# Keys and values of three token groups computed in blocks of 64 tokens sorted by head, instead of for all heads

## The chip, the cores and the metric

The kernel runs on one core of one Trainium2 chip. A core has a matrix engine (TensorE, PE in the profile, with its weight loads as PEld), a vector engine (VectorE, DVE), a scalar engine (ScalarE, ACT), a general engine (GpSimd, POOL) and a sequencer for transfers (SyncE, SP). The engines run side by side, each works through its own instructions in order, and semaphores order them among each other. Transfers are issued from a queue (here SP's, and POOL's for indirect ones) and carried out by 16 DMA engines. The metric is the device time of one execution in microseconds.

## The reference

Six layers follow each other on 8 sequences of 256 tokens with 512 features, each as `x = layernorm(x + layer(x))`: a differential attention, a long convolution with the context, a mixture of experts, a self-attention, a cross-attention with the context, and a routed attention. The change is about the last:

```python
gating = softmax(x @ W_gate.T)                    # 16 heads
indicator = one_hot(argmax(gating), 16)
gating_top1 = indicator * max(gating)
q, k, v = split(x @ W_qkv.T, 3)                   # each 16 heads of 32
k_shared = einsum('bth,bthd->btd', indicator, k)  # the key of the token's own head
v_shared = einsum('bth,bthd->btd', gating_top1, v)
att = einsum('bhqd,bkd->bhqk', q, k_shared) / sqrt(32)
y = einsum('bhqk,bkd->bhqd', softmax(causal(att)), v_shared)
```

Queries are wanted for all 16 heads. Of keys and values each token needs only 32 + 32 columns, those of the one head that its gate picks; all heads of the attention then use this one key and value per token. All arithmetic is in float32, but for small terms that carry the row maxima.

## The kernel before

The 2048 tokens are 16 tiles of 128 (`x[0]` to `x[15]`, in SBUF all the time); four tiles (two sequences) are a group, so there are four groups (`NG`). `by_columns` writes one product of 128 x 512 as four matmuls, 32 columns of the stationary operand each (L202); a block of four such steps contracts 512 features. `feature_block` makes 128 query features of a group, transposed; `token_block` makes 512 columns for one tile of tokens.

**The loop.** `causal_attention` (L1210) runs 32 units in the routed stage, one for each sequence and 128-column block of heads (four heads). A unit passes through stages that lie several units apart: `maxima` (scores ps_q on PE, L1264; copied by ACT, L1273; masked by POOL, L1275; row maxima by DVE, L1284), `split` and `turn` once per four units (the maxima as three bf16 terms, turned by PE, L1306), `weights` (scores again with the maxima subtracted, ps_k, L1327 and L1336; exponential on ACT, L1344; mask and a sum on POOL, L1345 and L1355) and `products` (ps_pv, L1370 and L1380; reciprocal on DVE, L1388; scaling, L1394). ps_q and ps_k share one PSUM buffer.

**Order.** PE, DVE, ACT and POOL follow in this stage exactly the order in which the code is written. `prepare` hands each group's projections to a queue as steps with a planned cost and a due slot (a slot is a unit); `fill` takes steps from the queue between the parts of a unit, `need` takes those that are due, and `at(slots, place, f)` puts a function at the start, the middle or the end of a later slot, or into the queue. SP's instructions are ordered by the framework's own scheduler, by dependencies and priorities, not by the written order.

**Projections of a group** (`prepare` in `routed_attention`, L1794): four turns of tiles (PE, copied by ACT, L221 and L222); the gate (L178, L190) with its softmax and one-hot (`softmax_small`, `first_max`) on DVE; four query blocks; four key blocks and four value blocks for all 16 heads, each 16 matmuls into ps_t, of which DVE then chooses the token's own head: a product with the one-hot row (L1825) and a sum over heads (L1831). The chosen keys are repeated four times (L1836) and turned (L1841, L1844). Group 0's turns, gate, three queries and keys stand ahead of the first unit; the other groups' in the four units ahead of their own first, the values later.

**The stages ahead.** The expert stage already sends tokens to slots sorted by expert: POOL scatters rows with indirect DMAs (L882), SP loads blocks by register (L1022, L1030), and POOL gathers results (L1189). The regions xs and ys are zeroed in the first attention by `clear_slots` (L738), 16 transfers of 4352 KB from SP's queue. At the end of that attention `load_context` (L414) and `turn_context` bring the context tiles in, turn them and write them back (ctx_d, L419), two tiles ahead of PE. The cross-attention's last normalisations (L1742, L155) end where the routed stage begins.

Of the kernel before, what the change touches and what calls it, by code (L numbers as in the profile page):

```python
# [17 lines left out]
F32 = mybir.dt.float32  # L18
BF16 = mybir.dt.bfloat16
AF = mybir.ActivationFunctionType  # L20
ALU = mybir.AluOpType
AX = mybir.AxisListType
PSUM = bass.MemoryType.PSUM

P = 128
B, S, D = 8, 256, 512
NT = B * S // P
TPG = 4
# [18 lines left out]
NE = (PH * 2 * P - E * (P - 1) - 1) // P + 1  # L47


@with_exitstack  # L50
def decoder_kernel(ctx: ExitStack, tc: tile.TileContext, a: dict, out: bass.AP):
# [43 lines left out]
    ctx_d = dram.tile([P, KB, B * S], F32, tag="ctx_d", name="ctx_d")  # L95

# [146 lines left out]
    def turned_group(work, pools, g):  # L243

        xT = []

        def step(ti):
            if ti == 0:
                xT.append(work.tile([P, KB, GT], F32, tag="xT", name="xT", bufs=1))
            turned(pools, xT[0][:, :, ti * P : (ti + 1) * P], x[g * TPG + ti])  # L250

        return xT, [(0, [(TR, lambda ti=ti: step(ti))]) for ti in range(TPG)]
# [439 lines left out]
    def experts(rt):  # L692
# [39 lines left out]
        def clear_slots(pool):  # L732
# [3 lines left out]
            for e in range(E):  # L736
                for region in (xs, ys):
# [5 lines left out]
                    )  # L743

# [461 lines left out]
        return clear_slots, load_experts, load_gu_last, router, blocks, combine, wide  # L1206
# [577 lines left out]
    def routed_weights(w):  # L1784
        g = 3 * D * KB
        load_w(w, g, a["L1_ffn_W_gate"], H1)
        nc.vector.memset(w[:, g + KB * H1 : g + KB * H1 + 32 - H1], 0.0)
        return load_w(w, 0, a["L1_ffn_W_qkv"], 3 * D), w[:, g:]

    def routed_attention(wqkv, wg):  # L1790

        idx = index_row(const, H1, "idx_h")

        def prepare(work, pools, g, at, here):  # L1794
# [5 lines left out]
            k4 = work.tile([P, TPG, 4, HD1], F32, tag="k4", name="k4")  # L1800
            ind = work.tile([P, TPG, H1], F32, tag="ind", name="ind")
            itop = work.tile([P, TPG, H1], F32, tag="itop", name="itop")

            part = work.tile([P, GT], F32, tag="gpart", name="gpart", bufs=1)

            def gate_parts():
                columns_by_block(
                    pools.tile([P, GT], F32, tag="mm", name="ps_g"), part, wg, H1, lambda k: xT[0][:, k, :]
                )

            def gates():
                pt = pools.tile([P, TPG, P], F32, tag="mm", name="pt_g")
                gate = work.tile([P, TPG, H1], F32, tag="gate", name="gate")
                sum_of_blocks(gate, pt, part)
                softmax_small(work, gate, H1)
                top = work.tile([P, TPG], F32, tag="top", name="top")
                first_max(work, gate, H1, idx, top, ind)
                nc.vector.tensor_tensor(
                    itop, ind, top.unsqueeze(2).broadcast_to([P, TPG, H1]), ALU.mult
                )  # L1820
# [12 lines left out]
            def key(ti, ps):  # L1833
                k = k4[:, ti]
                chosen(k[:, 0, :], ps, ind[:, ti, :])
# [9 lines left out]

            xT, need = turned_group(work, pools, g)
            need.append((0, [(MM, gate_parts)]))
            need.append((0, feature_block(pools, qT, xT, wqkv, 0, 0, HD1**-0.5)))
            need.append((0, [(TR, gates)]))
            need.append((0, feature_block(pools, qT, xT, wqkv, 0, 1, HD1**-0.5)))  # L1850
            for ti in range(TPG):
                need.append(
                    (0, token_block(pools, xT, wqkv, D, ti, lambda ps, ti=ti: key(ti, ps)))
                )
            need.append((0, feature_block(pools, qT, xT, wqkv, 0, 2, HD1**-0.5)))
            need.append((0, [(TR, keys_turned)]))
            for c in range(3, KB):
                need.append((c, feature_block(pools, qT, xT, wqkv, 0, c, HD1**-0.5)))
            for ti in range(TPG):
                need.append(  # L1860
                    (
                        5 + ti // 2 * (4 if g == NG - 1 else 2),
# [142 lines left out]
```

## Time and profile before

| | us |
|---|---|
| median of 3 runs | 2131.78 (2131.77 to 2133.14) |
| the profiled execution: time | 2132.13 |
| its span on the core | 2130.4 |
| routed stage (end of the cross-attention's PE work to the end of the span) | 347.8 |
| of it ahead of the first unit | 34.0 |
| PE busy in the routed stage | 307.1 |
| DVE busy there | 243.0 |

A row of a timeline gives start, duration, engine, line and operation, `out<-in`, and in brackets the idle time ahead of it and who ended it. A float32 matmul stands as two records in the profile, so 16 matmuls are 32 records. A row of a group gives the count after an x, then busy time and the mean of one in ns, then the idle time of the engine ahead of it with the releaser. A row of a DMA gives the number of transfers, KB of each, and the median time from issue to landing. `granted clock` is the share of PE's full clock.

### The profile page before, as it was taken

Reading aid. Unit: us, or ns where it says so; the run is one execution under the profiler, and the core shown is the slowest. Engines: PE = TensorE matmul, PEld = TensorE weight load, DVE = VectorE, ACT = ScalarE, POOL = GpSimd, SP = SyncE. Lnnn points to the kernel's source line nnn. Section 1 sums busy time; section 2 is a strip of 40 time slices with the busy share of each in tenths; the row PEclk is TensorE's granted clock in tenths of the full one; section 3 lists DMA queues with packets and bytes.
Section 4 is the critical chain, followed back from the end, with each engine's and each line's share of the span. In section 5 each row is a group of like instructions: output and inputs, shape, how many; then the busy total and the mean of one; then the engine's idle time right before and its main releaser. Section 6 shows DMA issues by size and latency. Waiting matters only on the chain. (4 is left out here: it accounts for less than half of the span.)

```text
span 2130.4 us, 46282 instructions
## 1 busy us (share of the span) xinstructions
PE 1985.9 (93%) x20206; PEld 1127.1 (53%) x20206; DVE 1272.5 (60%) x1935; ACT 604.1 (28%) x765; POOL 828.1 (39%) x919
## 2 busy tenths in 40 slices
PE   8979999879998999999969999998999999999995
PEld 5545555434443446656535554547787874344443
DVE  4677777658888964222235766565334343577787
ACT  4555555520010013211114433430110111333342
POOL 2677777637556833000034554332000000242443
PEclk9999999999999999999989999999999999999998
DMA  6899902235124145142132211002100100000000
GB/s 226 320 398 390 351 4 62 85 93 197 30 80 150 48 126 180 64 144 70 43 102 62 91 61 32 2 2 100 40 26 15 40 0 1 1 8 15 11 22 31
DMA packets 110073, 198.24 MB, mean 93 GB/s; under 512 B 7088, under 2 KB 30768, under 8 KB 109872
## 3 DMA queue, kind: packets, MB, share of 16 engines
q1 hardware_dynamic: 104752, 178.49, 24.1%
q0 software_dynamic: 5120, 16.78, 2.4%
q8 instruction: 161, 2.64, 0.5%
q14 instruction: 40, 0.33, 0.0%
HBM read 93.54 MB, written 112.20 MB: 97 GB/s over the span
## 5 line engine op out<-in xcount | busy, mean ns | idle before, releaser
L1388 DVE RECIPROCAL rsum<-ps_pv 128x256 f32<-128x256 f32 x128 | 224.5, 1754 | 223.8 <-PE ps_pv L1380 223.8
L172 PE MATMUL ps_y<-kv,wt 128*128 128x512 f32 x640 | 278.9, 594 | 5.9 <-DVE kv L597 2.7
L1344 ACT ACTIVATE pT<-ps_k 128x1536 f32<-128x1536 f32 x128 | 185.8, 1452 | 261.3 <-PE ps_k L1336 253.3
L1284 DVE TENSOR_REDUCE neg<-rows 128x12 f32<-128x1536 f32 x128 | 222.9, 1742 | 39.4 <-POOL rows L1275 39.4
L1273 ACT COPY rows<-ps_q 128x1536 f32<-128x1536 f32 x128 | 184.2, 1439 | 174.3 <-PE ps_q L1264 119.6
L1345 POOL TENSOR_SCALAR_AFFINE_SELECT pT<-pT 128x1024 f32<-128x1024 f32 x128 | 140.9, 1101 | 233.2 <-ACT pT L1344 233.2
L1275 POOL TENSOR_SCALAR_AFFINE_SELECT rows<-rows 128x1024 f32<-128x1024 f32 x128 | 141.0, 1102 | 213.0 <-ACT rows L1273 212.6
L172 PEld LDWEIGHTS ps_y<-kv,wt 128*128 128x128 f32 x640 | 120.0, 190 | 156.9 <-issue 135.9
L1355 POOL TENSOR_TENSOR pT<-pT 128x512 f32<-128x512 f32 x112 | 146.6, 1309 | 9.4
L1189 POOL DMA_INDIRECT w_l1x<-ys,slots x32 | 33.2, 1039 | 258.4 <-DMA ys<-y_m 250.8
L202 PE MATMUL ps_f<-xT,w_l1a 128*32 128x256 f32 x2048 | 121.7, 384 | 0.7 <-ACT xT L222 0.7
L202 PE MATMUL ps_t<-w_l1f,xT 128*32 128x512 f32 x1024 | 120.7, 603 | 0.0
L1097 PE MATMUL po_m<-dn,hT 128*128 (+1 forms) x216 | 98.7, 593 | 1.0 <-ACT hT L1087 1.0
L140 POOL TENSOR_SCALAR rstd<-bn_mv 128x1 f32<-128x1 f32 x80 | 16.8, 210 | 209.1 <-DVE bn_mv L146 203.3
L1380 PE MATMUL ps_pv<-pT,ones_v 128*32 128x256 f32 (+1 forms) x1152 | 83.9, 373 | 11.4 <-POOL pT L1355 11.4
L635 DVE TENSOR_REDUCE yc<-z 128x64 f32<-128x512 f32 x128 | 86.1, 673 | 5.6 <-POOL w_l1a L636 5.2
L202 PEld LDWEIGHTS ps_f<-xT,w_l1a 128*32 128x32 f32 x2048 | 62.1, 110 | 45.2 <-issue 7.0
L1264 PE MATMUL ps_q<-kz,qT 32*128 32x128 f32 x1536 | 63.2, 295 | 15.6 <-ACT pT L1344 13.4
L1264 PEld LDWEIGHTS ps_q<-kT,qT 32*128 32x128 f32 x1536 | 49.8, 190 | 47.9 <-issue 23.1
L1264 PEld LDWEIGHTS ps_q<-kz,qT 32*128 32x128 f32 x1536 | 50.7, 193 | 44.3 <-ACT pT L1344 31.8
L1076 DVE TENSOR_TENSOR h_b<-h_b,pg 128x352 f32<-128x352 f32 x36 | 18.7, 521 | 92.4 <-ACT h_b L1075 92.4
L1327 PE MATMUL ps_k<-qT,kT 32*128 32x256 f32 (+1 forms) x1024 | 67.9, 351 | 4.2 <-ACT rows L1273 3.0
(338 smaller groups left out, 3626.9 us busy)
## 6 DMA issues: line engine op xcount, KB each, us to landing
xs<-zero SPq DMA_DIRECT2D x8, 4352.0 KB, 32.4
ys<-zero SPq DMA_DIRECT2D x8, 4352.0 KB, 32.5
filters<-in_L_xattn_k SPq DMA_DIRECT2D x4, 2560.0 KB
first_h<-xs SPq DMA_DIRECT2D x36, 256.0 KB, 2.7
ys<-y_m SPq DMA_DIRECT2D x36, 256.0 KB, 2.0
gu<-in_L_ffn_gate_up_proj SPq DMA_DIRECT2D x3, 2816.0 KB, 19.7
wt<-filters SPq DMA_DIRECT2D x32, 256.0 KB, 2.8
x<-in_x SPq DMA_DIRECT2D x16, 256.0 KB, 6.5
```

The costliest lines, as they stand in the source:

```text
L172: nc.tensor.matmul(ps, lhsT=lhsT(k), rhs=rhs(k), start=(k == 0), stop=(k == n - 1))
L202: nc.tensor.matmul(ps[cs], lhsT=lhsT[:, cs], rhs=rhs, start=start, stop=stop)
L635: nc.vector.tensor_reduce(yc[:, lb], z, AX.X, ALU.add)
L1097: nc.tensor.matmul(po, lhsT=hT[:m, i, :], rhs=dn[i][:m, bass.ds(e, 1), :], start=(i == 0), stop=(i == len(FCH) - 1),)
L1264: nc.tensor.matmul(block[:, s, j, :], lhsT=q(rows, c, b * S + i * P, P), rhs=k(rows, c, b * S + keys * P, P), start=True, stop=True,)
L1273: nc.scalar.copy(d.rearrange("p j s k -> p s j k"), block)
L1275: nc.gpsimd.affine_select(out=rows, in_=rows, compare_op=ALU.is_ge, fill=-FAR, base=0, pattern=[[0, 8], [-1, P]], channel_multiplier=1,)
L1284: return lambda: nc.vector.tensor_reduce(neg[u // upb % 2][:, :, :, c], d, AX.X, ALU.max, negate=True)
L1344: nc.scalar.activation(p[:, 0:3].rearrange("p j s q -> p s j q"), block, AF.Exp)
L1345: nc.gpsimd.affine_select(out=p[:, 0:2].rearrange("p j s q -> p (j s) q"), in_=p[:, 0:2].rearrange("p j s q -> p (j s) q"), compare_op=ALU ...
L1355: nc.gpsimd.tensor_tensor(p[:, 3], p[:, 1], p[:, 2], ALU.add)
L1388: nc.vector.reciprocal(r, ps[:, 1, :])
```

## The change

The gates of all four groups are made at the start of the stage, in one softmax and one choice for all 16 tiles, with all turned tiles kept (four buffers instead of one). Group 0 gets its keys and values as before. The 12 tiles of groups 1 to 3 are handled by head:

- On DVE and PE (`add_up`, `place`) each token gets a slot in a list sorted by head, in which each head begins on a block of 64 rows; there are at most 40 blocks (`NV`). `which` holds each block's head.
- POOL scatters the rows of the 12 tiles to `sorted_x` in DRAM (`send`), which was zeroed in the first attention, behind xs and ys.
- SP loads for each double block (128 sorted rows, 20 of them) the rows, and for each of its two blocks the 32 key and 32 value columns of its head (128 KB, the address from `which` by register) out of `by_head`. `by_head` is a copy of the key and value weights in DRAM with each head's columns together; eight DRAM-to-DRAM copies of 2048 runs of 128 bytes make it. They depend on inputs alone, and in the built order they stand in SP's queue in the first attention: two behind the second context load and the router's weights, six behind the third context load.
- PE turns the 128 rows (L1973 in the listing of the changed kernel), ACT copies them, PE multiplies 64 columns in 16 matmuls; four double blocks share a PSUM tile, which ACT copies and SP writes to `kvd` in DRAM. Rows have three buffers, weights four.
- POOL gathers for each tile of a group the rows of `kvd` back in token order (`fetch`, four for each of groups 1 to 3, ahead of the group's first unit), and DVE repeats the keys and scales the values with the gate (`spread`).

What no longer exists is the choice out of 16 heads for these 12 tiles and their 24 key and value blocks. In the built order of the four engines nothing changes ahead of the routed stage. In SP's queue the sorted rows 0 to 5 are asked for one behind the other after the weights of double blocks 0 to 3; rows 7 stand behind the weights of double blocks 5 to 7, and rows 13 behind those of 12 and 13.

```diff
+VB = 64
+NV = (NT - TPG) * P // VB + H1
...
+            n = NV * VB // P
+            ins = nc.sync.dma_start(
+                out=sorted_x.rearrange("(p r) d -> p r d", p=P),
+                in_=zero.unsqueeze(1).broadcast_to([P, n, D]),
+            )
+            cleared.append(ins.ins.name)
...
+        for k in range(KB):
+            rows = a["L1_ffn_W_qkv"][k * P : (k + 1) * P, D:]
+            for c in range(2):
+                nc.sync.dma_start(
+                    out=by_head.rearrange("(e p) (k c d) -> k c p e d", p=P, k=KB, c=2)[k, c],
+                    in_=rows[:, c * D : (c + 1) * D].rearrange("p (e d) -> p e d", d=HD1),
+                )
...
+            def add_up():
+                nc.vector.memset(ahead[:, 0, :], 0.0)
+                for i in range(1, m):
+                    nc.vector.tensor_tensor(
+                        ahead[:, i, :], ahead[:, i - 1, :], o[:, i - 1, :], ALU.add
+                    )
+                nc.vector.tensor_tensor(count, ahead[:, m - 1, :], o[:, m - 1, :], ALU.add)
+
+            def place():
+                before, ones = masks
+                ps = pools.tile([P, m + 1, H1], F32, tag="mm", name="ps_pl")
+                nc.tensor.matmul(ps[:, m, :], lhsT=ones, rhs=count, start=True, stop=True)
+                nc.tensor.matmul(ps[:, :m], lhsT=before, rhs=o, start=True, stop=False)
+                nc.tensor.matmul(ps[:, :m], lhsT=ones, rhs=ahead, start=False, stop=True)
...
+                nc.vector.tensor_copy(slot, sj)
+                for i in range(m):
+                    at(i // 6, ("mid", "end")[i // 3 % 2], lambda i=i: send(i))
...
+            def send(i):
+                ins = nc.gpsimd.indirect_dma_start(
+                    out=sorted_x[:, :],
+                    out_offset=bass.IndirectOffsetOnAxis(ap=slot[:, i : i + 1], axis=0),
+                    in_=x[tiles[i]],
+                    in_offset=None,
+                )
+                for name in cleared:
+                    wait_for(ins.ins, name, "zeroes first")
+                gone.append(ins.ins.name)
...
+            def load(j):
...
+                wb = work.tile([P, 2, KB, 2 * HD1], F32, tag="wb", name="wb", bufs=4)
+                for i in range(2):
+                    e = w_of[j // 4][2 * (j % 4) + i]
+                    nc.sync.dma_start(
+                        out=wb[:, i].rearrange("p k c -> p (k c)"),
+                        in_=by_head[bass.ds(e, P), :],
+                    )
+                xs_j = work.tile([P, D], F32, tag="xs", name="xs_j", bufs=3)
+                ins = nc.sync.dma_start(out=xs_j, in_=sorted_x[j * P : (j + 1) * P, :])
+                for name in gone:
+                    wait_for(ins.ins, name, "all rows of a head")
+                rows[j] = xs_j, wb
...
+            def product(j):
+                if j % 4 == 0:
+                    ps.append(pools.tile([P, 4, 2 * HD1], F32, tag="mm", name="ps_kv"))
+                xT, (_, wb) = cols.pop(j), rows.pop(j)
+                for k in range(KB):
+                    for s in range(4):
+                        cs = slice(32 * s, 32 * s + 32)
+                        nc.tensor.matmul(
+                            ps[0][cs, j % 4, :],
+                            lhsT=xT[:, k, cs],
+                            rhs=wb[:, s // 2, k, :],
+                            start=(k == 0),
+                            stop=(k == KB - 1),
+                        )
...
+            if g == 0:
+                turns = [token_turns(work, pools, i) for i in range(NG)]
...
+                early += query(0) + parts[NG - 1] + totals[NG - 2 :] + query(1) + query(2) + adds
...
+                early += query(3) + places + keys[0] + keys[1] + keys[2] + keys[3]
+                early.append((TR, keys_turned))
+                need.append((0, early))
...
+                def begin_loads():
+                    for j in range(n - 2):
+                        load(j)
+                    for j in range(n):
+                        at(0, "due mid", (4 + 3 * j // n, steps[j : j + 1]))
+
+                at(2, "start", begin_loads)
+            else:
+                kv = work.tile([P, TPG, 2 * HD1], F32, tag="own", name="own")
+                first = 6 if g == 1 else 8 * g - 3
...
+                for ti in range(TPG):
+                    at(first - here, "end", lambda ti=ti: fetch(ti))
+                at(first + 1 - here, "mid", spread)
+                for c in range(KB):
+                    need.append((c, query(c)))
```

## The prediction

> **What bounds the kernel now.** I read the page's busy times and slices first, then the busy time by stretches of the last stage (the change puts almost all of its work there), then that stage's groups of instructions by form, and last the timelines of PE, DVE, POOL and SP around the places the change touches. The page gives the frame:
>
> ```profile
> span 2130.4 us, 46282 instructions
> PE 1985.9 (93%) x20206; PEld 1127.1 (53%) x20206; DVE 1272.5 (60%) x1935; ACT 604.1 (28%) x765; POOL 828.1 (39%) x919
> ```
>
> PE is the engine to relieve. The routed stage begins when PE ends the cross-attention at 1782.6 us. I cut it at the score products ps_q of L1264: the first at 1816.6, the seventh at 1852.7, the first of the last group at 2040.6, the last at 2083.1. The columns are length, then busy us and count of PE, PEld, DVE, ACT, POOL, then granted clock, DMA share, GB/s:
>
> ```profile
> 1782.60:1816.60 34.00, 30.02 (x260) 10.10 (x259) 13.28 (x31) 5.24 (x10) 0.74 (x2) 0.95 0.00 1
> 1816.60:1852.70 36.10, 32.73 (x392) 13.33 (x392) 19.00 (x20) 13.49 (x14) 8.93 (x8) 0.95 0.01 2
> 1852.70:1928.80 76.10, 73.47 (x1024) 32.60 (x1020) 55.29 (x76) 29.39 (x29) 29.22 (x28) 1.00 0.03 9
> 1928.80:2040.60 111.80, 106.23 (x1391) 46.30 (x1387) 83.63 (x123) 37.87 (x38) 39.12 (x42) 0.98 0.04 16
> 2040.60:2083.10 42.50, 40.61 (x676) 20.59 (x672) 36.07 (x48) 21.37 (x17) 24.07 (x24) 1.00 0.04 14
> 2083.10:2130.40 47.30, 24.01 (x412) 14.49 (x408) 35.73 (x47) 10.52 (x8) 16.46 (x23) 0.80 0.09 34
> ```
>
> See that PE fills 88 to 97% up to 2083.1, that DVE is second with 73 to 85% from 1852.7 on, and that the DMA queues are empty. In the groups of this stage, see which PE work goes, and what DVE keeps:
>
> ```profile
> L202 PE MATMUL ps_t<-w_l1f,xT 128*32 128x512 f32 x1024 | 120.7, 603 | 0.0
> ...
> L1388 DVE RECIPROCAL rsum<-ps_pv 128x256 f32<-128x256 f32 x32 | 56.0, 1749 | 26.1 <-PE ps_pv L1380 26.1
> L1284 DVE TENSOR_REDUCE neg<-rows 128x12 f32<-128x1536 f32 x32 | 55.7, 1742 | 9.0 <-POOL rows L1275 9.0
> ...
> L1831 DVE TENSOR_REDUCE v_r<-sel 128x32 f32<-128x512 f32 x16 | 16.9, 1058 | 0.5
> ...
> L1825 DVE TENSOR_TENSOR sel<-ps_t,itop 128x512 f32<-128x512 f32 x16 | 10.9, 684 | 7.8 <-PE ps_t L202 7.8
> ```
>
> **Removed.** Key and value blocks of groups 1 to 3: 24 of 32. Four blocks in a row stand in the PE timeline as
>
> ```profile
> 1797.97 13.92 PE L202 MATMUL ps_t<-w_l1f,xT 128*32 128x512 f32 x128
> ```
>
> so 3.48 us a block, 83.5 us of PE. On DVE 24 pairs of choose (0.69) and sum (1.06) go: 42 us. Queries, turns and gates stay and only move.
>
> **Added on PE.** 20 double blocks of 128 sorted rows, each four 128x128 transposes (0.55 us) and 16 matmuls of 64 columns. No row has 64 columns; the nearest, the values of the first attention, has the same tiles with 128 columns:
>
> ```profile
> 29.77 2.83 PE L202 MATMUL ps_v<-w_l,xT 128*32 128x128 f32 x96
> ```
>
> 96 records are 48 matmuls, so 0.94 us for 16; by columns half of it, 0.47. I take 0.9, since the 128x32 weight loads are as many. 20 x 1.45 = 29 us, placing matmuls 0.9. PE saves 53.6 us if it never waits: that is the ceiling, and it will wait.
>
> **Front, to the first ps_q.** All 16 turns, four gates, four queries, the placing and group 0's four key blocks now stand before it in the built order. ACT's first copy of a turn starts at 1786.0 as before (it follows the last DVE normalisation) and four take 2.05, so 18 copies end at 1795.2; then query 0, the last gate and its transposes to 1802.6; queries 1 to 3 (10.6) to 1813.2. Beside these DVE makes gates and running sums: 11 operations of 256 elements and waits for one on ACT (0.44 each by the 0.42 row of L192), then 13 small ones at 0.22 (spacing of the L1295/L1298 rows), 8.2 us, covered. After the placing matmuls (1814.1) DVE needs 20 small operations, two of 384 and three of 192 elements, 6.5 us to the slots, and 2.1 more for the blocks' heads; then four key choices (2.0 each) end at 1830.8, while PE's key blocks ended at 1828.0. PE waits 2.8, turns the keys, and ps_q starts at 1832.4: **+15.8 us** (12 to 20). The new wait is DVE's; behind it stand only pt_k and the first unit.
>
> **Middle, first to seventh ps_q.** Before: 36.1 us. After: four units with group 0's four value blocks take PE 4 x (0.88 + 3.5) = 17.6 us. The sends stand on POOL six behind the first affine select and six behind the second. The scatter's cadence is
>
> ```profile
> 668.44 0.96 POOL L882 DMA_INDIRECT xs<-xn,slots  x1 [0.30 <-issue]
> 669.71 1.29 POOL L882 DMA_INDIRECT xs<-xn,slots  x1 [0.30 <-issue]
> ...
> 672.56 0.96 POOL L882 DMA_INDIRECT xs<-xn,slots  x1 [0.30 <-issue]
> ```
>
> 1.27 us: select ends at 3.6, six sends 11.2, select 12.3, six sends 19.9, landing 2.7 later at 22.6. DVE's maxima 1 and 2 wait for these selects, without harm yet. SP's load of the first sorted rows waits for all twelve sends; behind it on SP stand the later head weights, the kvd writes and the output writes; PE waits for it. The nearest loads are
>
> ```profile
> first_h<-xs SPq DMA_DIRECT2D x36, 256.0 KB, 2.7
> ...
> wt<-filters SPq DMA_DIRECT2D x32, 256.0 KB, 2.8
> ```
>
> so rows arrive at 25.7 and PE idles 8 us. Then 20 steps of 1.45, plus two stalls: in SP's order sorted rows 7 and 13 stand behind weights that wait for products 3 and 9, so each comes 1.3 (issues) + 2.7 us after that product, where PE has 1.2 us of work: 2 x 2.8. Units 4, 5 and the first weights add 3.1, start-up 1. Cold clock: after its 2 us wait at 1834.9 one block step took 1.63 instead of 1.03 us and the clock of that stretch reads 0.95, so 3.5 us for the three gaps. 25.7 + 29 + 5.6 + 4.1 + 3.5 = 68: **+32 us**. Lower end: no wait at all, 17.6 + 29 + 3.1 = 50 (+14). Upper end: each step a lone load, 0.15 + 0.35 + 2.7 + 0.55 = 3.75 us, 25.7 + 75 + 7 = 108 (+72). I take 68 because three row buffers keep three loads in flight, and 512 KB a step need 1.4 us at the 380 GB/s of the zero-filling slices, under PE's 1.45.
>
> [...]
>
> **Rest, seventh ps_q to the end.** Before: 277.7 us. Per unit DVE keeps 1.74 + 1.75 + 0.42, per four units two normalisations (0.70 + 0.69 + 0.18 + 0.92 each) and a split (1.3), and 0.1 for spreading fetched rows: 5.6 us. PE keeps 0.88 + 1.19 + 1.03, queries 1.78 and 0.43 of transposes: 5.3. The stretch 2040.6 to 2083.1, seven units of 6.07 us at 95% of PE, shows how near the larger of the two a unit comes: 5.6 / 0.95 = 5.9. 25 units are 147.5; the tail keeps its 47.3 less 1.7 of choosing. Three fetches of four gathers occupy POOL 5.1 us each, behind the second unit's sum; affine selects queue behind them, and the spread, ahead of the next maximum on DVE, waits for landing (3.6 in the gather row of L1189). The spread's reciprocal is ready 7.5 us after the scores, the rows 11: 3 us each, 9 in all (0 to 20). 147.5 + 45.6 + 9 = 202: **-75.6 us** (-100 to -62).
>
> **Early stages.** Zeroing sorted_x (5.2 MB) adds 13.8 us to SP behind the zeroes that end at 248 (11.5 us per 4.35 MB); SP is idle from 261 to 336 and DMA empty, so it is covered. by_head has 16384 runs of 128 bytes; in the built order two of its eight copies fall into that gap, six between context loads 2 and 3. ctx_d with 512 runs issues in 0.52 us, so six take 12.4: load 3 leaves at 350 instead of 346 and is read at 358. At the mean of that stretch (10412 packets, 28.2% of 16 engines over 97 us: 42 ns each) they last 32 us and PE waits 14. I take 0 to 14, at 1.
>
> **Sum.** 15.8 + 32 - 75.6 + 1 = -27 us. The profiled execution took 2132.1 us (span 2130.4 and 1.7 around it, 0.3 above the median of 2131.8): **2105 us**.
>
> **Rivals.** (1) More is hidden: sends and loads keep ahead and units run at PE's 5.3. Empty DMA queues speak for it, the fixed order of 12 sends on POOL against; the ceiling of 53.6 gives 2079. (2) Loads overlap by half only: midway between 1.45 and 3.75, 2.6 us a step, 23 us more: 2128. For: transfers of 128 and 256 KB; against: the zero-filling rate. (3) Slower: SP's in-order queue lets one load at a time through. From 2.8 us a step on the gain is gone (27 / 20 above 1.45); at 3.75 the middle is 108, 40 above mine: 2145. For: two such places stand in SP's order; against: elsewhere three rows are asked for together.
>
> **How the numbers follow.** Forecast 0.60 (own range 2092 to 2118), rival 1 0.16, rival 2 0.13, rival 3 0.11. About 0.2% (4 us) is what this kernel's measurement can tell from no change. Rival 3 and a sliver of 2 are slower, 0.12; within 0.03; faster 0.85. The range takes in most of rival 1 and rival 2, and leaves out rival 3 and a rest of 0.05 below: 2077 to 2131.
>
> **What would show it.** Right: ps_t at L202's successor drops to 256 records; first ps_q some 16 us later in the stage; PE idle for about 8 us before the first transpose of sorted rows with a DMA as releaser; 1.4 to 2 us a step after that; units of 5.8 to 6 with DVE above 90%; short POOL holds at three gathers. Wrong: steps above 2.8 us, a PE wait near 358, units still above 6.5, or gathers that wait for kvd. Most open is the pace of the loads.

## The result: no gain, and where it went

The changed kernel takes 2138.59 us in the median of 12 runs (2133.22 to 2145.8), the kernel before 2131.47 us on the same chip (2128.9 to 2135.39): a ratio of 1.0035, 95% interval 1.0022 to 1.0048. The forecast was 2105, faster with 0.85.

Of the changed kernel one execution was profiled: 2134.01 us, span 2132.3. Against the profiled execution of before (span 2130.4) that is 1.9 us more, while the medians differ by 7.1. What the slower executions of the changed kernel spend on top was not profiled and stays open. All that follows is read from profiled executions, by stretches of the routed stage. Where nothing was changed these agree between kernels and chips to 0.3 us in most cases and to 2.2 at worst, while the time ahead of the routed stage differs by up to 22 us from chip to chip and execution to execution.

First the page of the changed kernel, busy time of the engines. PE had 1985.9 us before and DVE 1272.5.

```profile
PE 1942.7 (91%) x20164; PEld 1130.2 (53%) x20164; DVE 1235.9 (58%) x1890; ACT 616.0 (29%) x787; POOL 851.3 (40%) x945
```

PE does lose 43.2 us of work, of the 53.6 that the prediction named as the ceiling. Then the three stretches of the prediction, cut in the changed kernel at the end of the cross-attention on PE (1781.30), the first ps_q, the seventh ps_q and the end. Columns: length, busy us and count of PE, PEld, DVE, ACT, POOL, then granted clock, DMA share, GB/s.

```profile
1781.30:1830.38 49.08, 44.10 (x379) 18.56 (x378) 25.34 (x76) 13.82 (x26) 1.01 (x4) 1.00 0.08 23
1830.38:1915.71 85.33, 52.25 (x1024) 32.83 (x1024) 18.16 (x20) 23.03 (x32) 20.54 (x20) 0.78 0.49 155
1915.71:2132.30 216.59, 169.49 (x2691) 89.76 (x2684) 163.20 (x202) 93.08 (x80) 120.97 (x128) 0.90 0.07 24
```

| stretch | before | forecast | measured | error of the forecast |
|---|---|---|---|---|
| before the routed stage | 1782.6 | +1 | 1781.3 (-1.3) | 2.3 too much |
| front, to the first ps_q | 34.0 | +15.8 | 49.1 (+15.1) | 0.7 too much |
| middle, to the seventh ps_q | 36.1 | +32 | 85.3 (+49.2) | 17.2 too little |
| rest, to the end | 277.7 | -75.6 | 216.6 (-61.1) | 14.5 too little |

The sum is +1.9. PE's work went, but PE is busy only 52 of 85 us in the middle (61%, before 33 of 36, 91%) and 169 of 217 in the rest (78%, before 244 of 278, 88%). The saved work came back as waiting, in two places.

**The middle.** POOL's timeline in the changed kernel shows the sends. Columns: start, us, engine, line, operation, and in brackets the idle time before it with what ended it.

```profile
1832.95 1.10 POOL L1287 TENSOR_SCALAR_AFFINE_SELECT rows<-rows 128x1024 f32<-128x1024 f32 x1 [47.91 <-ACT rows L1285]
1834.22 1.08 POOL L1927 DMA_INDIRECT sorted_x<-x,slot  x1 [0.18 <-issue]
1837.28 0.97 POOL L1927 DMA_INDIRECT sorted_x<-x,slot  x1 [1.98 <-DMA sorted_x<-x,slot]
1840.69 0.96 POOL L1927 DMA_INDIRECT sorted_x<-x,slot  x1 [2.44 <-DMA sorted_x<-x,slot]
...
1867.18 0.96 POOL L1927 DMA_INDIRECT sorted_x<-x,slot  x1 [1.99 <-DMA sorted_x<-x,slot]
```

A send starts 2.94 us after the one before in most cases (2.92 to 3.41), not 1.27, and the bracket says why: it waits for the landing of its predecessor. The twelve take 34 us instead of the forecast 16. PE has its units and values until 1850 and then stands:

```profile
1872.85 2.90 PE L1973 MATMUL pt<-ident,xs_j 128*128 128x128 f32 x12 [22.95 <-DMA xs_j<-sorted_x]
...
1879.99 0.65 PE L1973 MATMUL pt<-ident,xs_j 128*128 128x128 f32 x4
1880.58 0.65 PE L1985 MATMUL ps_kv<-wb,xsT 128*32 128x64 f32 x32
...
1885.86 1.09 PE L1973 MATMUL pt<-ident,xs_j 128*128 128x128 f32 x4 [3.46 <-DMA xs_j<-sorted_x]
...
1900.38 1.09 PE L1973 MATMUL pt<-ident,xs_j 128*128 128x128 f32 x4 [3.53 <-DMA xs_j<-sorted_x]
```

22.95 us, where 8 were forecast. The steps themselves then take 1872.85 to 1915.71, 42.9 us with the units between them; the forecast's last terms (29 + 5.6 + 4.1 + 3.5) make 42.2. A warm step is 0.59 for the transposes and 0.59 for the 16 products.

**The rest.** The lines of PE and DVE about the first fetch of gathered rows and about the second:

```profile
1925.38 0.23 PE L1348 MATMUL ps_k<-negT,take 32*128 32x128 bf16 x4
1931.19 1.12 PE L2035 MATMUL pt_k<-ident,k 128*128 128x128 f32 x4 [5.57 <-DVE k L2112]
1932.23 3.64 PE L208 MATMUL ps_f<-xT,w_l1f 128*32 128x512 f32 x16
...
1983.00 0.86 PE L1382 MATMUL ps_pv<-pT,v_r 128*32 128x256 f32 x16 [2.10 <-POOL pT L1357]
1984.42 0.81 PE L1392 MATMUL ps_pv<-pT,ones_v 128*32 128x256 f32 x8 [0.56 <-POOL pT L1367]
```

```profile
1930.26 0.87 DVE L2112 COPY k<-own 128x512 f32<-128x512 f32 x1 [3.39 <-DMA own<-kvd,slot]
...
1982.49 0.75 DVE L2112 COPY k<-own 128x512 f32<-128x512 f32 x1 [3.65 <-DMA own<-kvd,slot]
1983.16 1.35 DVE L2115 TENSOR_TENSOR v_r<-own,top 128x128 f32<-128x128 f32 x1
1984.43 1.74 DVE L1296 TENSOR_REDUCE neg<-rows 128x12 f32<-128x1536 f32 x1
```

DVE stands for the landing of each fetch, with the next maximum (neg) behind it in its order; at the first fetch PE's turn of the keys waits behind DVE too, and the sixteen ps_f matmul records after it take 3.64 instead of 1.92 us: the granted clock is 0.50 from 1931.19 to 1935.87, right behind that wait, and 1.00 in an undisturbed unit. At the second and third fetch PE waits for POOL, whose select and sum of pT stand behind the four gathers: 2.10 and 0.56 us, then 2.07 and 0.56. DVE's late maximum reaches PE one unit later (0.65 and 0.59 us of waiting for `terms`). From ps_q to ps_q a unit is 5.85 us in undisturbed places; the three that hold a fetch are 14.24, 10.23 and 10.14, and each unit after them 6.7 to 6.8.

### The profile page after: what moved, and what is told of

The parts are those of the page before. It is cut to its first block, busy times and chain, and to the rows that moved or that the text cites. A ratio compares the mean times of both kernels' runs of the same rounds, so it can differ in the third digit from the quotient of the medians.

```text
span 2132.3 us, 46481 instructions
## 1 busy us (share of the span) xinstructions
PE 1942.7 (91%) x20164; PEld 1130.2 (53%) x20164; DVE 1235.9 (58%) x1890; ACT 616.0 (29%) x787; POOL 851.3 (40%) x945
## 5 line engine op out<-in xcount | busy, mean ns | idle before, releaser
L1287 POOL TENSOR_SCALAR_AFFINE_SELECT rows<-rows 128x1024 f32<-128x1024 f32 x128 | 141.2, 1104 | 209.5 <-ACT rows L1285 208.9
L208 PEld LDWEIGHTS ps_f<-xT,w_l1a 128*32 128x32 f32 x2048 | 62.2, 111 | 45.6 <-issue 7.7
L1276 PE MATMUL ps_q<-kT,qT 32*128 32x128 f32 x1536 | 62.6, 293 | 12.6 <-ACT pT L1356 7.7
```

The costliest lines, as they stand in the source:

```text
L208: nc.tensor.matmul(ps[cs], lhsT=lhsT[:, cs], rhs=rhs, start=start, stop=stop)
L1276: nc.tensor.matmul(block[:, s, j, :], lhsT=q(rows, c, b * S + i * P, P), rhs=k(rows, c, b * S + keys * P, P), start=True, stop=True,)
L1287: nc.gpsimd.affine_select(out=rows, in_=rows, compare_op=ALU.is_ge, fill=-FAR, base=0, pattern=[[0, 8], [-1, P]], channel_multiplier=1,)
```

## The experiments

The times of each experiment are compared with the kernel before, run beside it on the same chip. The table gives their stretches (us, from each run's profile); front begins at the end of the cross-attention on PE. gathers_earlier and four_weights have one execution each, without an interval. In free_sends and sends_ahead the profiled execution is the longest of those measured (2138.11 us with a median of 2132.82, and 2142.14 with 2134.48).

| kernel | front | middle | rest | sum | ratio to before (95%) |
|---|---|---|---|---|---|
| before | 34.0 | 36.1 | 277.7 | 347.8 | 1 |
| changed | 49.1 | 85.3 | 216.6 | 351.0 | 1.0035 (1.0022 to 1.0048) |
| early_alone | 34.2 | 36.1 | 277.9 | 348.2 | 1.0004 (0.9994 to 1.0014) |
| free_sends | 49.1 | 73.0 | 216.8 | 338.9 | 0.9938 (0.992 to 0.9957) |
| rows_first | 49.1 | 86.5 | 216.6 | 352.2 | 1.0013 (0.9997 to 1.0028) |
| gathers_apart | 49.1 | 85.3 | 209.5 | 343.9 | 0.9983 (0.9971 to 0.9996) |
| gathers_earlier | 49.1 | 87.5 | 208.8 | 345.4 | one execution |
| sends_ahead | 59.2 | 62.0 | 217.4 | 338.6 | 0.9947 (0.9932 to 0.9963) |
| start_apart | 49.1 | 61.3 | 209.9 | 320.3 | 0.987 (0.9854 to 0.9887) |
| steps_sooner | 49.1 | 64.5 | 203.2 | 316.8 | 0.989 (0.9873 to 0.9907) |
| third_apart | 59.3 | 64.8 | 202.7 | 326.8 | 0.9912 (0.9891 to 0.9934) |
| four_weights | 59.3 | 51.8 | 205.9 | 317.0 | one execution, work left out |
| weights_5 | 59.2 | 63.1 | 211.3 | 333.6 | 0.9937 (0.9919 to 0.9955) |
| rows_4 | 59.2 | 59.6 | 211.4 | 330.2 | 0.9928 (0.9911 to 0.9944) |

### early_alone: the parts ahead of the routed stage

```diff
+            nc.sync.dma_start(out=sorted_x.rearrange("(p r) d -> p r d", p=P),
+                in_=zero.unsqueeze(1).broadcast_to([P, 40 * 64 // P, D]))
...
+        for k in range(KB):          # the eight copies into by_head
+            for c in range(2):
+                nc.sync.dma_start(out=by_head..., in_=rows...)
```

> The kernel before, with the zeroing of sorted_x and the eight copies into by_head added at their places and nothing else; nobody reads them. Theory (both lie in gaps of SP and of the DMA engines): the time is that of the kernel before, within 2 us (ratio 0.999 to 1.001), and the first attention stages end when they did. Rival (the 16384 runs of 128 bytes hold a context load, or the zeroes the filters): 3 to 14 us more (ratio 1.0015 to 1.0065).

Measured: 1.0004, interval 0.9994 to 1.0014, and the cross-attention ends at 1781.8 us against 1782.6. The theory holds: zeroes and copies are free here. So the loss of the changed kernel lies in the routed stage as far as the profiles show it.

### free_sends: the sends without the order between them

```diff
                 for name in cleared:
                     wait_for(ins.ins, name, "zeroes first")
+                tc.declare_no_dep(ins.ins, group="sorted", reason="every row has its own slot")
+                tc.add_to_no_dep_group("sorted", ins.ins)
                 gone.append(ins.ins.name)
+                nc.gpsimd.memset(apart, 0.0)
```

> The twelve sends no longer wait for each other's landing; a 128x1 memset on POOL stands between them. In the changed kernel they left 2.94 us apart, and TensorE idled 22.95 us before the first transpose of sorted rows. Theory (the order between the sends alone set that): they leave 1.3 to 1.5 us apart, the last leaves near 1853 instead of 1867, the idle falls to 8.5 us (7 to 10) and the time by 14.5 us, to about 2124 (2120 to 2127). Rival 1 (a scatter takes 2.9 us whatever the order says): the cadence stays above 2.5 us and the time stays at 2134 to 2139. Rival 2 (the rows come sooner, but then the loads of rows and weights fall behind the steps): the idle falls, but the stretch from the first to the seventh ps_q shortens by less than 8 us.

POOL's and PE's lines in free_sends:

```profile
1851.79 0.97 POOL L1928 DMA_INDIRECT sorted_x<-x,slot  x1 [0.18 <-issue]
1852.76 0.12 POOL L1939 MEMSET apart<- 128x1 f32 x1
1853.06 0.96 POOL L1928 DMA_INDIRECT sorted_x<-x,slot  x1 [0.18 <-issue]
```

```profile
1874.35 2.79 PE L1977 MATMUL pt<-ident,xs_j 128*128 128x128 f32 x12 [2.05 <-DMA xs_j<-sorted_x]
```

The cadence is 1.27 us, so nothing in the scatter itself needs 2.9: the order between the sends set it. (The memset that now stands between two sends takes 0.12 us; the expert stage has its 1.27 without one.) PE's wait ahead of the steps falls from 22.95 to 2.05 us and the middle by 12.3 us to 73.0 (14.5 were expected). Against before the kernel is now 0.6% faster, 12 us in the medians on its chip. That the idle fell below the expected 8.5 and the middle by less goes with two gaps ahead of it: ACT's copies of scores stood 9.98 and 7.50 us, so that a part of PE's idle time moved there. The first of the two ("remote" stands where the profile knows no instruction that released the wait) is taken up in the last section with its like:

```profile
1859.03 1.44 ACT L1285 COPY rows<-ps_q 128x1536 f32<-128x1536 f32 x1 [9.98 <-remote]
```

### rows_first: rows ahead of weights in SP's order

```diff
-                wb = ...; for i in range(2): nc.sync.dma_start(out=wb[:, i]..., in_=by_head[...])
                 xs_j = ...; ins = nc.sync.dma_start(out=xs_j, in_=sorted_x[j * P : (j + 1) * P, :])
+                wb = ...; for i in range(2): nc.sync.dma_start(out=wb[:, i]..., in_=by_head[...])
```

> In SP's order each load of sorted rows now stands ahead of the two weight loads of its own step instead of behind them. The changed kernel stood still 3.46, 3.53, 1.10 and 1.14 us in the steps for rows. Theory (rows stand behind weights whose buffer is not free): these four go, the twenty steps take about 35 us instead of 42.9 and the time falls by 7 to 9 us, to about 2130 (2127 to 2133). Rival (the loads themselves are too slow for the steps, 384 KB or more per 1.2 us): the stalls return at the weights, and the steps stay above 40 us, the time at 2136 or more.

Measured: the middle is 86.5, not shorter. The two long stalls of 3.5 us are gone, but more short ones stand in their place, 12.5 us in all against 10.1. PE's lines:

```profile
1901.41 0.63 PE L1973 MATMUL pt<-ident,xs_j 128*128 128x128 f32 x4 [2.05 <-DMA xs_j<-sorted_x]
1905.67 0.63 PE L1973 MATMUL pt<-ident,xs_j 128*128 128x128 f32 x4 [0.53 <-DMA xs_j<-sorted_x]
1909.03 0.63 PE L1973 MATMUL pt<-ident,xs_j 128*128 128x128 f32 x4 [2.15 <-DMA xs_j<-sorted_x]
```

The theory falls: the place of the rows behind their own step's weights in SP's queue is not what costs. The rival is right about the time and not about where the stalls come back, which is at the rows again.

### gathers_apart and gathers_earlier: the fetch of the last two groups

gathers_apart spreads the four gathers over POOL's order:

```diff
-                    at(first - here, "end", lambda ti=ti: fetch(ti))
+                    slot, place = first - here, "end"
+                    if g > 1:
+                        slot, place = ((0, "end"), (1, "mid"), (1, "end"), (2, "start"))[ti]
+                    at(slot, place, lambda ti=ti: fetch(ti))
```

gathers_earlier leaves them together and moves them a unit ahead:

```diff
-                    at(first - here, "end", lambda ti=ti: fetch(ti))
+                    at(first - (g > 1) - here, "end", lambda ti=ti: fetch(ti))
```

> For the last two groups the four gathers no longer stand in one row on POOL: one stands at the end of the unit before, two in the unit, one at the start of the next. In the changed kernel each of these two fetches made one interval of ps_q 10.2 us instead of 5.9, the next 6.7, with 3.65 us of VectorE waiting for the gathered rows and 5.1 us of POOL held. Theory (holding POOL and waiting for the landing is the cost): the two intervals fall to 7 or less, the time by 6 to 9 us, to about 2131 (2128 to 2134). Rival (the spread's two VectorE operations, 2.1 us, and the slack that the chain of scores, selects and products lacks are the cost): the intervals stay above 9 us and the time falls by less than 2 us.

> The changed kernel with the four gathers of each of the last two groups still in one row on POOL, but one unit earlier, so that the gathered rows have landed before the spread. Of the 10.2 us interval of ps_q, theory 1 (POOL held for 5.1 us, the select of the next scores behind it, is the cost) leaves one interval of 9 us or more at each of the two, now a unit earlier; theory 2 (VectorE's wait of 3.65 us for the landing is the cost) lets both fall to 7 us or less. By the first the stretch from the seventh ps_q to the end stays at 214 to 218 us, by the second it falls to 209 to 211.

DVE's lines at the second fetch in gathers_apart, and then in gathers_earlier, the latter with PE's wait there:

```profile
1988.82 0.42 DVE L1406 TENSOR_TENSOR yT_b<-ps_pv,rsum 128x256 f32<-128x256 f32 x1
1989.45 0.43 DVE L2112 COPY k<-own 128x512 f32<-128x512 f32 x1 [0.20 <-DMA own<-kvd,slot]
1989.79 0.28 DVE L2115 TENSOR_TENSOR v_r<-own,top 128x128 f32<-128x128 f32 x1
```

```profile
1983.57 0.42 DVE L1406 TENSOR_TENSOR yT_b<-ps_pv,rsum 128x256 f32<-128x256 f32 x1
1983.91 0.42 DVE L2112 COPY k<-own 128x512 f32<-128x512 f32 x1
...
1979.72 0.86 PE L1382 MATMUL ps_pv<-pT,v_r 128*32 128x256 f32 x16 [1.62 <-POOL pT L1357]
```

DVE's wait of 3.65 us goes in both. In gathers_apart the two intervals are 7.07 and 7.03 instead of 10.23 and 10.14, and the rest is 209.5 instead of 216.6: 7.1 us, as expected. gathers_earlier still holds POOL for the 5.1 us of four gathers, and its rest is 208.8. Its two intervals are 8.38 and 7.53, so 1.6 to 2.5 us above 5.9 remain of the 4.3, and at the first of them PE still waits for POOL, 1.62 and 0.50 us. The stretch speaks for theory 2 (209 to 211 was expected); the intervals lie between the two (7 or less, 9 or more). So the hold of POOL is a part of the cost in any case. How the part that went divides between the wait for the landing, the place in the unit and the clock (granted 0.83 in the changed kernel's two intervals) is not shown. The spread itself is shorter as well, 0.42 and 0.28 us instead of 0.75 and 1.35.

### sends_ahead and start_apart: when the sends begin

sends_ahead issues the twelve sends right where the slots are ready, with free_sends' change; start_apart hangs them on the start of the first unit instead, and has gathers_apart's change too.

```diff
                 for i in range(m):
-                    at(i // 6, ("mid", "end")[i // 3 % 2], lambda i=i: send(i))
+                    send(i)                                   # sends_ahead
+                    at(0, "start", lambda i=i: send(i))       # start_apart
```

> As free_sends, and all twelve sends stand on POOL ahead of the first affine select, right behind the slots (ready at 1819.5 in the changed kernel). Theory (the start of the steps follows the last send): the sends run from about 1820 to 1837, the rows are there by 1843 and TensorE does not idle before the steps, as its units and values reach to 1850; the time falls by 20 to 23 us against the changed kernel, to about 2117 (2113 to 2121). The first select comes some 4 us later, at no cost. Rival (the late select, and the maxima behind it on VectorE, hold the units): TensorE idles 5 us or more elsewhere in this stretch and the time is no better than free_sends.

> The sends free of each other and all at the start of the first unit, now behind the four key choices of VectorE in the order of the program, and the gathers of the last two groups apart. The routed stage of the changed kernel took 49.1 us to the first ps_q, 85.3 to the seventh, 216.6 to the end: 351.0, before 347.8. Theory (in sends_ahead VectorE's fourth key choice was bound to the sends only by standing behind them in the program): the first part is 49 to 51 again, the second 60 to 64, the third 209.5: 321, 27 us under the kernel before, ratio 0.986 to 0.989. Rival (POOL's scatters hold VectorE whatever the order): the first part is 57 or more again, or that wait appears at another VectorE instruction, and the ratio is 0.991 or more.

sends_ahead: the middle falls to 62.0 as expected, but the front grows by 10.1, and the kernel is no better than free_sends (0.9947 and 0.9938). It is not the select that is late. DVE's fourth key choice stands, and PE's turn of the keys behind it:

```profile
1847.61 0.25 DVE L2034 COPY k<-k 128x96 f32<-128x96 f32 x1
1857.79 0.69 DVE L2023 TENSOR_TENSOR sel<-ps_t,ind 128x512 f32<-128x512 f32 x1 [9.93 <-remote]
```

I took this for the order of the program; start_apart was made for that. On another chip its front is 49.1 again, the middle 61.3 and the rest 209.9, all three as the theory said, and 2102.68 us against 2130.76, 0.987 (0.9854 to 0.9887). Its windows:

```profile
1779.68:1828.79 49.11, 44.08 (x379) 18.60 (x378) 25.41 (x76) 13.82 (x26) 10.11 (x21) 1.00 0.16 55
1828.79:1890.06 61.27, 51.43 (x1024) 32.09 (x1024) 18.32 (x20) 23.21 (x32) 13.08 (x16) 0.86 0.61 190
1890.06:2100.00 209.94, 163.86 (x2688) 87.09 (x2684) 163.04 (x202) 92.99 (x80) 121.20 (x128) 0.93 0.07 24
```

The explanation by program order is wrong all the same: third_apart, four_weights, weights_5 and rows_4 (below) have the sends in the order of start_apart and ran on other chips, and all four show DVE's wait again (9.8 to 9.9 us, fronts of 59.2).

### four_weights, weights_5, rows_4: what paces the loads

Three variants of start_apart. four_weights loads head weights for the first four steps only and multiplies all later rows with those:

```diff
-                for i in range(2):
+                wb = ... if j < 4 else first4[j % 4]
+                for i in range(2 if j < 4 else 0):
```

weights_5 and rows_4 change one buffer count, and take one of the two buffers of the gathered rows for it:

```diff
+                wb = work.tile(..., tag="wb", name="wb", bufs=5)        # weights_5
+                xs_j = work.tile(..., tag="xs", name="xs_j", bufs=4)    # rows_4
```

> As start_apart, but only the first four steps load head weights; the later sixteen use those four tiles again, so that the keys and values of most blocks are made with another head's weights: the loading is left out, the products are not. In start_apart the steps stood still for rows 9.1 us in all, 3.66 the longest, each load landing 3.4 us after its issue. Theory (the rows stand in SP's queue behind weights whose buffers are not free, and share the DMA engines with them): the stalls fall under 2 us, the second part from 61.3 to 52 to 55. Rival (three row buffers ask for a row only three steps ahead, too late by itself): the stalls stay at 6 us or more and the second part at 58 or more.

> start_apart with five buffers for head weights instead of four (the gathered rows keep one buffer instead of two, to make room). start_apart: 9.1 us of stalls for rows in the steps, 61.3 us in the second part, and four_weights, without the later weights, 51.8 with 5.7 us of stalls. Theory (the rows stand in SP's queue behind weights that wait for a buffer): one buffer more lets the loads run one step further ahead, the two long stalls of 2.3 and 3.7 us shrink, the second part is 56 to 59. Rival (the transfers of weights and rows share the DMA engines and SP's issues, so that a buffer changes nothing): 60 to 63.

> start_apart with four buffers for sorted rows instead of three (the gathered rows again with one buffer). By the theory of weights_5 the rows still stand behind weights, so that the second part stays at 60 to 63. Rival (a row is asked for too late, only three steps ahead): the second part is 56 to 59 here, and not with weights_5. If both stay at 60 or more, the pace of SP's issues and of the transfers is what is left.

Measured: without the later weights the middle is 51.8 us, 9.5 less, as the theory had it. The stalls for rows fall from 9.1 to 5.7 us, not under 2; the longest is 1.78 instead of 3.66, and PE's granted clock in that stretch is 0.96 instead of 0.86. The window of the middle in four_weights, to be set against the second line of start_apart's above:

```profile
1852.34:1904.14 51.80, 45.90 (x1025) 28.17 (x1025) 18.33 (x20) 22.73 (x32) 8.08 (x8) 0.96 0.36 100
```

PE's busy time itself falls by 5.5 us for the same matmuls: at the lower clock the same step takes longer. So of the 9.5 us more than half is clock. PE's lines in start_apart show where it fell:

```profile
1859.29 0.63 PE L1977 MATMUL pt<-ident,xs_j 128*128 128x128 f32 x4 [2.27 <-DMA xs_j<-sorted_x]
...
1862.54 1.09 PE L1977 MATMUL pt<-ident,xs_j 128*128 128x128 f32 x4 [0.39 <-DMA xs_j<-sorted_x]
...
1874.30 1.09 PE L1977 MATMUL pt<-ident,xs_j 128*128 128x128 f32 x4 [3.66 <-DMA xs_j<-sorted_x]
```

From about 1 us behind the wait of 2.27, and at once behind the one of 3.66, the granted clock is 0.50 for some 6 us each (1860.5 to 1866.6 and 1874.3 to 1880.4); in four_weights, with no wait above 1.78, it is 1.00 from 1872 to 1904. No threshold follows from this: in rows_first the clock is 0.50 behind a wait of 2.15 and 1.00 behind one of 2.05. The two kernels ran on different chips, and the sends of four_weights end ahead of its middle (its front holds DVE's wait); weights_5 and rows_4 share that front, and four_weights is 11.3 and 7.8 us shorter than they are in the middle.

One buffer more does not do it: 63.1 us with five for weights, 59.6 with four for rows, and 10.8 and 9.7 us of stalls (1.8 of the latter for weights). Both predictions of 56 to 59 fail, rows_4 by little. This does not rule the buffers out. SP's order changed with rows_4: within the steps eight loads of weights in a row (1868.87 to 1874.15) now stand ahead of the rows that PE then waits 4.13 us for, where start_apart has at most six. And more buffers of both kinds at once were not run, though in the changed kernel's steps SP waits 10.2 of the 42.9 us for PE to release a buffer of rows or weights. What paces the loads, buffers, SP's order and issues or the transfers, stays open.

### steps_sooner and third_apart: the fetch of the second group

Both take start_apart and move the steps of the sorted rows and the gathers of the second group forward; third_apart begins the steps a unit later than steps_sooner.

```diff
-                        at(0, "due mid", (4 + 3 * j // n, steps[j : j + 1]))
+                        at(0, "due mid", (2 + 4 * j // n, steps[j : j + 1]))   # steps_sooner
+                        at(0, "due mid", (3 + 3 * j // n, steps[j : j + 1]))   # third_apart
-                at(2, "start", begin_loads)
+                at(1, "start", begin_loads)
...
+                    if g == 1:
+                        slot, place = ((1, "mid"), (1, "mid"), (1, "end"), (2, "start"))[ti]
...
-                at(first + 1 - here, "mid", spread)
+                at(2, "end", spread) if g == 1 else at(first + 1 - here, "mid", spread)
...
-                    at(0, "fill", [(TR, keys_turned)])
+                    at(1, "mid", keys_turned) if g == 1 else at(0, "fill", [(TR, keys_turned)])   # third_apart
```

> As start_apart, and the twenty steps of the sorted rows are due from the third unit to the sixth instead of the fifth to the seventh, so that kvd is written earlier, and the gathers of the second group stand a unit earlier too, two and two. In the changed kernel its fetch made one interval of ps_q 14.2 us instead of 5.9, with 5.57 us of TensorE waiting. Theory (that fetch stood on the path only because its place in the order was right behind the last step): the interval falls to 7 or less, and the time by 6 to 9 us against start_apart, ratio 0.982 to 0.985. Rival (the steps, begun sooner, wait for their loads all the longer): the seventh ps_q comes 6 us or more later than there, and nothing is gained.

> As steps_sooner, but the twenty steps are due from the fourth unit to the sixth, behind the sends with more room, the gathers of the second group start two and two in the sixth unit, the spread stands at the end of the seventh, and the keys are turned in the middle of the eighth. start_apart took 61.3 us in the second part and 209.9 in the third; steps_sooner 64.5 and 203.2. Theory (the two gains and losses are independent: the fetch off the path is worth 6.7 us, and steps begun when their rows are there cost nothing): 61 to 63 and 202 to 204, 5 us or more under start_apart, ratio 0.982 to 0.986. Rival (a unit that follows the steps waits for VectorE and POOL, whichever order is taken): the sum of the two parts stays above 268, the ratio at 0.986 or more.

PE's line of the second group's keys in steps_sooner:

```profile
1903.10 0.65 PE L2039 MATMUL pt_k<-ident,k 128*128 128x128 f32 x4 [1.74 <-DVE k L2116]
```

The wait for the spread falls from 5.57 to 1.74 us, the interval from 14.2 to 8.2, and the rest to 203.2; in third_apart it is 202.7. That is the value of this fetch off the path: 6.7 us, with 1.74 of waiting left. But the middle grows by 3.3 and 3.5 us, to 64.5 and 64.8; in steps_sooner 2.1 of it are PE's waits for ACT in the units that follow the steps at once (1.56 and 0.55). Net, the stretches of steps_sooner's profiled execution are 3.5 us shorter than start_apart's; its median is not (2106.46 in a range of 2098.55 to 2110.15, and 2102.68 for start_apart). Their intervals overlap, so which is better is not settled. In third_apart the theory's 61 to 63 for the middle fails; its ratio, 0.9912, holds DVE's wait of 9.9 us; its stretches without that wait would sum to about 317.

## Why the prediction was wrong, step by step

- **Early parts, +1 (0 to 14).** Right: -1.3 in the profile, 1.0004 alone. The 14 us of the upper end did not come.
- **Front, +15.8 (12 to 20).** Right, +15.1. PE waited 1.60 us for DVE's last key and 0.68 for ACT where I had 2.8 for DVE.
- **Middle, the twelve sends.** This is the step that failed first: "select ends at 3.6, six sends 11.2 ... landing 2.7 later at 22.6". The cadence of 1.27 came from the sends of the expert stage. The row was read rightly, but it belonged to scatters that the kernel's expert stage declares independent of each other (`tc.declare_no_dep(ins.ins, group=group, reason=why)`, with the reason "every token has its own slots"); the new sends lack that declaration, and each waits for its predecessor to land: 2.94 us. The last send leaves 32.96 us after the first instead of some 15, and the first transpose starts 42.5 us after the first ps_q instead of 25.7. free_sends shows it: with the declaration the cadence is 1.27, and 2.05 us of idle are left in place of 22.95. The prediction's own sum for this stretch, with 1.27, is 68; free_sends measured 73.0, with the two waits of ACT in it that no term of the sum has.
- **Middle, the steps.** Right in size, 42.9 us against 42.2, but with two errors that cancel, which is luck. I charged two stalls of 2.8 to the places of rows 7 and 13 in SP's order. They came, 3.46 and 3.53, but rows_first removes that order and saves nothing. Warm steps are shorter than I had them (1.17 against 1.45) and the waits for loads longer: 10.1 us, with a granted clock of 0.81 in these 43 us. Mean traffic there was 224 GB/s; I had argued with the 380 of the zero-filling slices.

On that rate "DMA: Bandwidth & Descriptors" of the Trainium skill, section Bandwidth, gives 138 GB/s for a transfer of 64 KB and 341 for one of 1 MB, issued from GpSimd. The 224 of these loads of 128 and 256 KB, issued from SP, lies between the two; it is a mean over a stretch in which the queue also waited for buffers, so it does not test the page's figures.

- **Rest, -75.6 (-100 to -62).** Wrong by 14.5 us, just outside its range. The 25 intervals of ps_q that I had at 5.9 each with 9 us for three fetches, 156.5, measured 172.6; the tail was 44.0 against 45.6. The failing term is "3 us each, 9 in all (0 to 20)": the three intervals with a fetch exceed 5.9 by 8.3, 4.3 and 4.2, the ones after them by 0.8 to 0.9 each, 19.4 together. I counted one late reciprocal for each fetch. I left out that PE's turn of the second group's keys stands right behind the spread at the first fetch (5.57), that PE waits 2.7 us at each of the other two for POOL, where I had named selects behind the gathers without a price of their own, that the work after these waits runs on a lower clock (0.50 and 0.83), and what the maximum that I named behind the spread does to the unit after it. The remaining 5.7 us of the excess are spread over the other units; the largest, an interval of 9.04, is 7.05 in most of the later runs. With all three fetches moved the rest measured 203.2 (steps_sooner), close to the forecast's 202, but with intervals of 6.4 us in the mean (159.3 / 25) where I had 5.9 and 9 us for fetches. So 5.9 is what an undisturbed unit takes, not the mean. Its reason was not DVE alone: DVE was busy 75% of the rest, not over 90%. From 1967.68 to 1973.53 both engines are full (PE 5.85 us, DVE 5.83), from 1973.53 to 1979.37 PE is (5.84) and DVE is not (4.28); I had 5.3 for PE.
- **The rivals.** None of the three named what happened. Rival 3 (2145) came nearest to the median, but the steps did not run at 3.75 us. Its turning point, 27 us of loss, was reached by two other things: 17 at the sends and 14.5 in the rest.

So the saving that I forecast can be had on one chip: start_apart, with the sends free and early and two fetches off the path, is 1.3% faster than before, 28 us in the medians there, where the forecast had 27. That it is the same number is partly chance, as the middle is now below my sum and the rest above it. Its order was not run unchanged on the two chips with the waits of the last section; third_apart, weights_5 and rows_4, which differ from it in steps and gathers or in buffers, are 0.6 to 0.9% faster there.

## What to carry to other kernels

A duration taken from another place of the trace brings its conditions along. Before a cadence is carried over, read the source lines of both places for what orders their transfers: here one declaration made the difference between 1.27 and 2.94 us, twelve times, ahead of everything. Where work is taken from the busiest engine, list what each remaining round trip through DRAM (send, load, fetch) has queued behind it on every engine, and give it its lead before the work is removed; once the engine has gaps, its clock can fall too and a part of the saving goes with it (granted clock 0.78 in the middle of the changed kernel, 0.95 before).

## What was not expected of the hardware

With sends at a cadence of 1.27 us, another engine stood still on two chips for no reason that the profile or the program shows. In all five kernels with twelve sends in one row that ran on one of these two chips, DVE stood 9.8 to 9.9 us ahead of its fourth key choice, which in the built order waits only for PE's product, done long before; it went on as the last send landed (in sends_ahead at 1857.79; SP's loads that wait for all sends were issued from 1857.46). In free_sends, with two rows of six, it was ACT instead (9.98 and 7.50). On a third chip the two kernels with the same order (start_apart, steps_sooner) show no such wait in their profiled executions. The waits named "remote" occur elsewhere too on those two chips, on ACT and DVE, 2 to 9 us each, in rows_first and gathers_apart as well, whose sends are slow, and there the kernel before took 2138 to 2145 us instead of 2131. All eight profiles of those two chips have such waits of 2 us and more; none of the other six (before, changed, early_alone, gathers_earlier, start_apart, steps_sooner) has one. So in these runs they go with the chip, and the sends at most decide where they fall. What it is that the engines wait for stays open; no run tells it.
